# Sums of a GpSimd-added pair, issued later in TensorE's queue of a four-layer selective-scan kernel

## Chip, cores and metric

The kernel runs on one core of a Trainium2 chip. The metric is the device time of one execution in microseconds. The kernel before takes 22,061.91 us, the median of three runs (22,050.39 to 22,083.94).

## What is computed

Four layers are applied to a tensor of 4 images of 64x64 positions and 128 channels. Layers 0, 1 and 3 are selective-scan blocks, layer 2 is a gated block without a scan. The scan blocks take nearly all the time. Inside one, 256 channels are scanned along 4,096 positions in K = 4 directions, with N = 16 states for every channel:

```python
def step(h, t):
    dt_t, u_t, B_t, C_t = t
    h = h * jnp.exp(dt_t[..., None] * A) + (dt_t * u_t)[..., None] * B_t[:, :, None, :]
    y = jnp.einsum('bkdn,bkn->bkd', h, C_t)
    return (h, y)
```

So each state needs a decay (exp of delta times A), a driving term (delta times u times B, called the B product below), the recurrence itself, a multiplication by C, and the sum over the 16 states. Around the scans stand layer norms, projections, a 3x3 depthwise convolution, a gate and an MLP.

## The kernel before, in words

Twelve turns (4 images by 3 scan layers) are run, each with 4 directions of 8 chunks of 512 positions: 384 chunks. A chunk is cut into 8 periods, `i` = 0 to 7. A period has one group of four states (`q = i // 2`) and one half of the 256 channels on the 128 partitions. Two periods of the same `q`, an even one and the odd one after it, are called a pair here. There are 3,072 periods, 1,536 pairs.

The order of all instructions is written out by hand, in the loop over the periods (from L983). Each engine takes its instructions in that order. One period does this:

- ScalarE makes the decays of the next period (`decay`, L908), two states at a time ("sides" 0 and 1), and copies the driving term into PSUM (`lift`, L916).
- TensorE makes the B products of the first two states of the next period (`pair_db`, eight matmul instructions of L899 into the tile `dbp`, which has one buffer). VectorE makes those of the last two (L1048, L1049).
- VectorE runs four scans (L924), 128 x 512 each.
- GpSimd multiplies by C, two states in one instruction (`times_c`, L936, into a tile `hc` of four buffers). In even periods it then adds the two products of the sides (L938).
- TensorE sums over the states, by multiplying with an identity and accumulating in a PSUM bank for each half (`add_up`, L951; one sum is one call of it and two matmul instructions). An odd period has four sums (calls 0 to 3). An even one has two (calls 2 and 3), of the products that GpSimd has added. The last sum of a half appends it to the list `full`, and VectorE later takes the bank over (`leave`, L962 or L964).

In between stand the steps of other work, at four places in a period. `other(0)` stands after the first scan, `other(1)` after the B products of the next period, `other(2)` after the third scan and `other(3)` at the end. They hand out the norms, projections, MLP and convolution of the neighbouring turns, one kind of step at a time. A matmul step and the ScalarE, VectorE or GpSimd step that takes its result mostly stand at different places. All these matmuls write one PSUM tile, `gap`, with one buffer. `piece(2 * i)` after the B products and `piece(2 * i + 1)` at the end of a period give out the preparation of the next chunk (`prologue`, L814). Ten of the sixteen numbers have a piece; of those at the end of an odd period, number 3 (`i` = 1) has the projection `ps_x` (L835, in chunks of the forward directions), whose copy by ScalarE (L837) stands at the next place, and number 11 (`i` = 5) has four transposes of the tile `du` into `ps_duT` (L865), copied by ScalarE at L867.

On TensorE, from the B products issued in an odd period to those issued in the next even period, the order is: the pieces and steps of `other(1)` and `other(2)`; the two sums of the even period's pair (L951 x4 in the profile); the piece at the period's end and the steps of `other(3)`; in the next period the steps of `other(0)`; one sum of the odd period (L951 x2); the next B products (L899 x8). In the other half, at the end of an even period, three sums of the odd period before it stand together (L951 x6).

Of the kernel before, what the change touches and what calls it, by code (L numbers as in the profile page):

```python
# [77 lines left out]
def cost(step):  # L78

    return getattr(step, "matmuls", 0) or (0.05 if step is empty else 0.25)  # L80
# [6 lines left out]
def alike(a, b):  # L87
    return empty in (a, b) or hasattr(a, "matmuls") == hasattr(b, "matmuls")


def when(place):

    chunk, place = divmod(place - 1, 4 * len(ROOM))
    i, number = divmod(place, 4)
    return chunk + (sum(ROOM[:i]) + ROOM[i] * number / 4) / sum(ROOM)
# [3 lines left out]
def vss_stack_kernel(ctx: ExitStack, tc: tile.TileContext, x: bass.AP, weights, out: bass.AP, n_batch=B, layers=(0, 1, 2, 3)):  # L99
# [667 lines left out]
    for turn, (e, i) in enumerate(turns):  # L767

        for nth, k in enumerate((1, 3, 0, 2) if turn else (0, 1, 3, 2)):
            for ci in range(NCH):  # L770
                s = SimpleNamespace(turn=turn, e=e, v=wt[i], layer=i, nth=nth, k=k, ci=ci)
# [17 lines left out]
    def meanwhile(turn):  # L789

        chunk, end = 4 * 8, 4 * 8 * (per_turn - 2) - 4
        if not turn:

            first = [(row, n * chunk, (n + 1) * chunk - 2) for n, row in enumerate(opening[4:])]
            rest = combine(1, psums), combine(3, psums), *between(turns[1][0], None, 0, psums)
            return first + spaced(rest, first[-1][2], end)
        rows = after(*turns[turn - 1])
        if turn + 1 == len(turns):

            last = [(row, n * chunk + 8, (n + 1) * chunk + 8) for n, row in enumerate(after(*turns[turn]), 3 * NCH + 1)]  # L800
            return spaced(rows, 8, last[0][1]) + last
        if turns[turn + 1][1] == 0:
            rows += between(turns[turn + 1][0], None, 0, psums)
        return spaced(rows, 8, end)
# [4 lines left out]
    def scans(pool, ring, deep, psum):  # L809
# [60 lines left out]
        def spread(s, q, b):  # L870

            rows_of, at, count = ((s.bb, CQ * q + 2, CQ - 2), (s.cb, CQ * q, CQ))[b]
            rows_of[q] = pool.tile([P, count, CH], F32, tag="bc"[b] + "b", name="bc"[b] + "b")
            row = R + b * N + at
            nc.sync.dma_start(
                out=rows_of[q], in_=s.xd_d[s.k // 2 : s.k // 2 + 1, row : row + count].to_broadcast([P, count, CH])
            )

        def place(s, i):


            q = i // 2
            return q, (i + q + s.flip) % 2
# [19 lines left out]
        def decay(s, i, side):  # L903
            q, m = place(s, i)
            da = ring.tile([P, 2, CH], F32, tag="da", name="da")
            for j in range(2):
                n = CQ * q + 2 * side + j
                nc.scalar.activation(da[:, j], s.delta[:, m], AF.Exp, scale=s.v["a"][:, s.k, m, n : n + 1])  # L908
            return da
# [5 lines left out]
        def lift(s, i):  # L915
            nc.scalar.copy(dv[i % 2], s.du[:, place(s, i)[1]])  # L916

        def scan(s, i, side, j, da, db):
            q, m = place(s, i)
            if j == 0:  # L920
                s.h[i, side] = deep.tile([P, 2, CH], F32, tag="h", name="h")
            n = CQ * q + 2 * side + j
            init = 0.0 if s.first else s.state[:, m, n : n + 1]
            nc.vector.tensor_tensor_scan(  # L924
                s.h[i, side][:, j, s.step], da[:, j, s.step], db[:, s.step], init, ALU.mult, ALU.add
            )

        def save(s, i, side):
            if not s.last:
                q, m = place(s, i)  # L930
                n = CQ * q + 2 * side
                nc.scalar.copy(s.state[:, m, n : n + 2].unsqueeze(2), s.h[i, side][:, :, s.end : s.end + 1])  # L932
# [7 lines left out]
        def add_up(s, i, *calls):  # L940


            q, m = place(s, i)
            start, end = (0, 7) if m == s.flip else (1, 6)
            for call in calls:
                opens = i == start and call == (2 if i in PAIRED else 0)
                if opens:
                    setattr(s, f"yp{m}", psum.tile([P, CH], F32, tag=f"yp{m}", name="yp"))
                side, j = divmod(call, 2)
                closes = i == end and call == 3  # L950
                nc.tensor.matmul(getattr(s, f"yp{m}"), ident, s.hc[i, side][:, j], start=opens, stop=closes)  # L951
                if closes:
                    full.append((s, m))
# [17 lines left out]
        s = chunks[0]  # L971
# [9 lines left out]
        da = [decay(s, 0, side) for side in range(2)]  # L981
        pro = None
        periods = [(s, i) for s in chunks for i in range(8)]  # L983
        before, full = None, []
        for at, (s, i) in enumerate(periods):
            then = periods[at + 1] if at + 1 < len(periods) else None
            if i == 0:
                nxt = chunks[at // 8 + 1] if at // 8 + 1 < len(chunks) else None
                if nxt:
                    pro, nxt.dt = prologue(nxt), s.dt  # L990
                s.state = pool.tile([P, 2, N], F32, tag="state", name="state") if s.first else before[0].state
                if at % (8 * per_turn) == 0:
                    segments = [
                        SimpleNamespace(todo=steps, done=0, dense=True, total=len(steps), frm=frm, to=to)

                        if to - frm <= 4 * 8
                        else SimpleNamespace(
                            todo=steps, done=0, dense=False, total=sum(map(cost, steps)), frm=when(frm), to=when(to)
                        )
                        for steps, frm, to in meanwhile(s.turn)  # L1000
                    ]

            def piece(number):

                if nxt and number in PIECES:
                    next(pro)

            def other(number):

                place = at % (8 * per_turn) * 4 + number  # L1010
                for g in segments:
                    gone = place if g.dense else when(place)
                    while g.todo and g.done < g.total * (gone - g.frm) / (g.to - g.frm):
                        step = g.todo.pop(0)
                        g.done += 1 if g.dense else cost(step)
                        step()

                        if gone < g.to and not g.dense and (step is empty or g.todo and not alike(step, g.todo[0])):
                            break

            da_next = [None, None]
            spreads = (s, i // 2 + 1) if i < 7 else (nxt, 0)
            if i % 2 == 0 or not spreads[0]:
                spreads = None
            if then:
                da_next[0] = decay(*then, 0)
            if before:
                save(*before, 1)
            if spreads:
                spread(*spreads, 0)  # L1030
            scan(s, i, 0, 0, da[0], s.db[:, :, 0])
            other(0)
            scan(s, i, 0, 1, da[0], s.db[:, :, 1])
            times_c(s, i, 0)

            if before and i % 2 == 0:
                add_up(*before, 0)
            if then:
                pair_db(*then)
            piece(2 * i)  # L1040
            other(1)
            if spreads:
                spread(*spreads, 1)
            if then:
                da_next[1] = decay(*then, 1)
            save(s, i, 0)
            du, db = dv[i % 2], dv[1 - i % 2]
            nc.vector.tensor_mul(db, du, s.bb[i // 2][:, 0])  # L1048
            nc.vector.tensor_mul(du, du, s.bb[i // 2][:, 1])  # L1049
            scan(s, i, 1, 0, da[1], db)  # L1050
            other(2)
            scan(s, i, 1, 1, da[1], du)
            times_c(s, i, 1)
            if then:
                lift(*then)

            q, half = (i + 2 + i % 2) // 2, 1 - i % 2
            if q < 4:
                diagonals(s, q, half)
            elif nxt:  # L1060
                diagonals(nxt, q - 4, half)
            if i < 2 and full:
                leave(*full.pop(0))
            if before:
                add_up(*before, *((2, 3) if i % 2 else (1, 2, 3)))
            piece(2 * i + 1)
            other(3)
            da = da_next
            before = (s, i)
            if then and then[0].turn != s.turn:  # L1070
                assert not any(g.todo for g in segments)
        save(*before, 1)
        add_up(*before, 0, 1, 2, 3)
        while full:
            leave(*full.pop(0))
# [96 lines left out]
```

## Time and profile before

| what | value |
|---|---|
| median of three runs | 22,061.91 us |
| the profiled execution | 22,072.22 us |
| its span, first to last instruction | 22,070.4 us |
| granted TensorE clock, mean | 0.963 |
| VectorE busy | 19,479.8 us, 88% |
| GpSimd busy | 19,266.5 us, 87% |
| ScalarE busy | 18,587.9 us, 84% |
| TensorE (matmul) busy | 19,694.9 us, 89% |
| one pair of periods, span / 1,536 | 14.37 us |

How to read it: busy time is that of instructions on the engine itself; waiting at a semaphore is not in it. A line of the profile names a group of instructions by its line in the kernel, its engine and the tiles as output<-inputs. The view of the waits says which instruction sat idle before it started, what ended that idle time, how much in total, how often, and the longest one. PEld is the weight load that goes with a matmul.

### The profile page before, as it was taken

What the parts mean: (1) busy time and instruction counts of PE and PEld (TensorE: products, weight loads), DVE (VectorE), ACT (ScalarE), POOL (GpSimd) and SP (SyncE); (2) the same over time, 40 slices, a digit from 0 to 9 for tenths busy, and PEclk for the clock granted to TensorE, in tenths of its full rate; (3) what the DMA queues carried; (4) which work ended last, traced back from release to release, by engine and by line L of the source; (5) the groups of instructions that cost most, each with busy time, mean ns of one, the idle gap of its engine ahead of it and who ended that gap; (6) DMA issues with size and microseconds to landing.
All of it is one profiled execution on the core that took longest, in us unless ns stands there. A gap on an engine that the chain in (4) does not pass through costs nothing. (4 is left out here: it accounts for less than half of the span.)

```text
span 22070.4 us, 216982 instructions
## 1 busy us (share of the span) xinstructions
PE 19694.9 (89%) x58234; PEld 10511.8 (48%) x58234; DVE 19479.8 (88%) x20186; ACT 18587.9 (84%) x40022; POOL 19266.5 (87%) x8862
## 2 busy tenths in 40 slices
PE   7898998898889889889989988989988988898897
PEld 3444444444444444444444444444444444444443
DVE  5999999999888888899889899989988888889996
ACT  6888888888888888888888888888888888888887
POOL 5999899899888888888889888988988888889996
PEclk9999999999999999999999999999999999999999
DMA  4444444444335434434534544444443453354342
GB/s 109 147 149 146 135 144 149 136 139 151 130 131 139 142 128 140 146 133 145 144 138 144 145 141 140 141 147 134 142 149 127 137 143 137 131 140 145 140 144 101
DMA packets 2437559, 3060.10 MB, mean 139 GB/s; under 512 B 1753840, under 2 KB 1790064, under 8 KB 2238192
## 3 DMA queue, kind: packets, MB, share of 16 engines
q1 hardware_dynamic: 2436336, 3046.22, 44.4%
q8 instruction: 472, 7.73, 0.1%
q14 instruction: 751, 6.15, 0.1%
HBM read 2784.41 MB, written 261.49 MB: 138 GB/s over the span
## 5 line engine op out<-in xcount | busy, mean ns | idle before, releaser
L936 POOL TENSOR_TENSOR hc<-h,cb 128x1024 f32<-128x1024 f32 x6144 | 14399.4, 2363 | 2276.5 <-DVE h L924 1113.1
L951 PE MATMUL yp<-hc,ident 128*128 128x512 f32 x18432 | 9062.1, 618 | 688.3 <-POOL hc L938 546.8
L908 ACT ACTIVATE da<-delta,w 128x512 f32<-128x512 f32 x12288 | 8148.0, 713 | 543.5 <-DVE h L924 530.5
L924 DVE TENSOR_TENSOR_SCAN h<-da,state,dbp 128x512 f32<-128x512 f32 x5376 | 6573.3, 1262 | 818.9 <-PE dbp L899 576.0
L899 PE MATMUL dbp<-diag,duT 128*128 128x256 f32 x24576 | 6012.6, 388 | 652.4 <-DVE h L924 560.1
L924 DVE TENSOR_TENSOR_SCAN h<-da,state,dv 128x512 f32<-128x512 f32 x5376 | 6589.4, 1264 | 0.0
L899 PEld LDWEIGHTS dbp<-diag,duT 128*128 128x128 f32 x24576 | 4675.2, 193 | 2921.3 <-issue 1673.1
L951 PEld LDWEIGHTS yp<-hc,ident 128*128 128x128 f32 x18432 | 3483.6, 196 | 4999.1 <-issue 3656.8
L891 ACT ACTIVATE diag<-ident,bt 128x128 f32<-128x128 f32 x12288 | 3952.1, 402 | 0.0
L938 POOL TENSOR_TENSOR hc<-hc 128x1024 f32<-128x1024 f32 x1536 | 3624.1, 2359 | 120.4
L1048 DVE TENSOR_TENSOR dv<-dv,bb 128x512 f32<-128x512 f32 x3072 | 2088.3, 680 | 945.9 <-ACT dv L916 730.3
L916 ACT COPY dv<-du 128x512 f32<-128x512 f32 x3072 | 1799.1, 586 | 984.6 <-DVE h L924 977.1
L1049 DVE TENSOR_TENSOR dv<-dv,bb 128x512 f32<-128x512 f32 x3072 | 2118.4, 690 | 0.0
L444 PE MATMUL gap<-halo,cw 128*128 128x512 f32 x3456 | 1750.8, 604 | 5.9 <-DVE cen L281 2.2
L924 DVE TENSOR_TENSOR_SCAN h<-da,dbp 128x512 f32<-128x512 f32 x768 | 891.1, 1202 | 250.7 <-PE dbp L899 166.9
L859 POOL TENSOR_TENSOR du<-delta,xs 128x512 f32<-128x512 f32 x768 | 979.9, 1276 | 31.8 <-ACT delta L847 31.8
L842 PE MATMUL ps_dt<-xd,dt_w 8*128 8x512 f32 x1536 | 881.2, 654 | 130.2 <-ACT delta L845 78.2
L932 ACT COPY state<-h 128x2 f32<-128x2 f32 x5376 | 964.3, 179 | 0.0
L444 PEld LDWEIGHTS gap<-halo,cw 128*128 128x128 f32 x3456 | 628.1, 191 | 654.8 <-issue 617.8
L924 DVE TENSOR_TENSOR_SCAN h<-da,dv 128x512 f32<-128x512 f32 x768 | 893.8, 1204 | 0.0
L845 ACT ACTIVATE delta<-ps_dt,w 128x512 f32<-128x512 f32 x768 | 524.9, 683 | 103.0 <-PE ps_dt L842 98.2
L865 PEld LDWEIGHTS ps_duT<-ident,du 128*128 128x128 f32 x3072 | 383.7, 142 | 321.9 <-issue 255.8
(122 smaller groups left out, 11686.6 us busy)
## 6 DMA issues: line engine op xcount, KB each, us to landing
cb<-xd_d SPq DMA_DIRECT2D x1536, 1024.0 KB
bb<-xd_d SPq DMA_DIRECT2D x1536, 512.0 KB
xs<-x_row_d SPq DMA_DIRECT2D x192, 512.0 KB
xs<-x_col_d SPq DMA_DIRECT2D x192, 512.0 KB
x_col_d<-down SPq DMA_DIRECT2D x192, 256.0 KB
x_row_d<-wide SPq DMA_DIRECT2D x96, 512.0 KB
y_d<-y_sb SPq DMA_DIRECT2D x96, 512.0 KB
y<-y_d SPq DMA_DIRECT2D x96, 512.0 KB
```

Source lines behind the costliest of these rows:

```text
L444: nc.tensor.matmul(z.ps, z.cw[:, m, t, :], z.halo[c][:, dy : dy + RPC, dx : dx + W], start=(t == 0), stop=(t == 8),)
L859: nc.gpsimd.tensor_mul(s.du[:, m], s.delta[:, m], s.xs[:, m])
L891: nc.scalar.activation(s.diag[q][:, t, :, j], ident, AF.Copy, scale=s.bt[:, t, CQ * q + j : CQ * q + j + 1])
L899: nc.tensor.matmul(s.db[:, t * P : (t + 1) * P, :], s.duT[:, t, m, :], s.diag[q][:, t], start=True, stop=True)
L908: nc.scalar.activation(da[:, j], s.delta[:, m], AF.Exp, scale=s.v["a"][:, s.k, m, n : n + 1])
L916: nc.scalar.copy(dv[i % 2], s.du[:, place(s, i)[1]])
L924: nc.vector.tensor_tensor_scan(s.h[i, side][:, j, s.step], da[:, j, s.step], db[:, s.step], init, ALU.mult, ALU.add)
L936: nc.gpsimd.tensor_mul(hc, s.h[i, side], s.cb[i // 2][:, 2 * side : 2 * side + 2, :])
L938: nc.gpsimd.tensor_add(hc, hc, s.hc[i, 0])
L951: nc.tensor.matmul(getattr(s, f"yp{m}"), ident, s.hc[i, side][:, j], start=opens, stop=closes)
L1048: nc.vector.tensor_mul(db, du, s.bb[i // 2][:, 0])
L1049: nc.vector.tensor_mul(du, du, s.bb[i // 2][:, 1])
```

## The change

The two sums of an even period (calls 2 and 3) are no longer issued at the end of the odd period after it. They are issued in the following even period, after the steps of `other(0)`, directly before the one sum of the odd period that stood there already, and so directly before the next B products. Three sums now stand together there. To reach the pair two periods back, the loop keeps it in `earlier`. The first pair of the program is treated in the same manner as the others, and the last pair's sums follow the loop.

```diff
@@ -981,7 +981,7 @@
-        before, full = None, []
+        earlier, before, full = None, None, []
@@ -1033,7 +1033,8 @@
-            if before and i % 2 == 0:
+            if earlier and i % 2 == 0:
+                add_up(*earlier, 2, 3)
                 add_up(*before, 0)
             if then:
                 pair_db(*then)
@@ -1061,15 +1062,16 @@
             if i < 2 and full:
                 leave(*full.pop(0))
-            if before:
-                add_up(*before, *((2, 3) if i % 2 else (1, 2, 3)))
+            if before and i % 2 == 0:
+                add_up(*before, 1, 2, 3)
             piece(2 * i + 1)
             other(3)
             da = da_next
-            before = (s, i)
+            earlier, before = before, (s, i)
             if then and then[0].turn != s.turn:
                 assert not any(g.todo for g in segments)
         save(*before, 1)
+        add_up(*earlier, 2, 3)
         add_up(*before, 0, 1, 2, 3)
```

The number and kind of the instructions stay the same. The order changes on TensorE alone; VectorE, ScalarE, GpSimd and the queue of the transfers keep theirs.

## The prediction

> **What bounds the kernel now.** I read the page first.
>
> ```profile
> span 22070.4 us, 216982 instructions
> ...
> PE 19694.9 (89%) x58234; PEld 10511.8 (48%) x58234; DVE 19479.8 (88%) x20186; ACT 18587.9 (84%) x40022; POOL 19266.5 (87%) x8862
> ...
> L938 POOL TENSOR_TENSOR hc<-hc 128x1024 f32<-128x1024 f32 x1536 | 3624.1, 2359 | 120.4
> ```
>
> No engine is the bound alone: four stand between 84% and 89%. The time is set by how they wait for each other, so the view of the waits comes next (who waits <- for whom: us in total, times, longest).
>
> ```profile
> DVE h L924 <- PE dbp L899: 742.8, 557, 8.6
> DVE dv L1048 <- ACT dv L916: 730.3, 328, 7.5
> ...
> PE yp L951 <- POOL hc L938: 546.8, 361, 7.3
> ...
> ACT xd L837 <- PE ps_x L835: 248.3, 107, 8.4
> ...
> POOL hc L936 <- PE yp L951: 174.4, 97, 6.5
> ...
> PE yp L951 <- POOL hc L936: 121.9, 194, 1.2
> ...
> ACT duT L867 <- PE ps_duT L865: 104.9, 103, 5.2
> ```
>
> TensorE waits 546.8 us at the first of the sums that move, for GpSimd's addition. VectorE, which does the scans, waits mainly for TensorE's B products (742.8) and for ScalarE's copy (730.3). ScalarE is late in part because it waits for TensorE's preparation of the next chunk (248.3 and 104.9), whose matmuls stand right behind the sums that move. Two stretches of the timeline show both sides (start, us, engine, line; in brackets the idle time and what ended it). The first:
>
> ```profile
> 7114.69 3.78 PE L951 MATMUL yp<-hc,ident 128*128 128x512 f32 x4 [5.16 <-POOL hc L938]
> ...
> 7118.27 1.91 PE L696 MATMUL gap<-t,wg 128*128 128x512 f32 x2
> ...
> 7120.28 0.69 ACT L700 ACTIVATE c<-gap,wg 128x512 f32<-128x512 f32 x1 [5.02 <-PE gap L696]
> ...
> 7123.05 1.28 DVE L924 TENSOR_TENSOR_SCAN h<-da,state,dbp 128x512 f32<-128x512 f32 x1 [4.43 <-PE dbp L899]
> ```
>
> The sums wait 5.16 us for GpSimd; the step L696, which needs nothing of them, waits behind them; ScalarE waits for that step, and VectorE for the B products. The second:
>
> ```profile
> 7131.27 1.88 PE L951 MATMUL yp<-hc,ident 128*128 128x512 f32 x4
> ...
> 7133.71 1.13 PE L261 MATMUL gap<-res,mean 128*128 128x512 f32 x2 [0.56 <-POOL res L683]
> ...
> 7135.53 1.89 PE L899 MATMUL dbp<-diag,duT 128*128 128x256 f32 x8
> ...
> 7137.52 1.28 DVE L924 TENSOR_TENSOR_SCAN h<-da,state,dbp 128x512 f32<-128x512 f32 x1 [0.45 <-PE dbp L899]
> ```
>
> Here the sums are ready and fill 1.88 us in which the step L261 could not have run, since its input arrives at 7133.7. With the sums behind it, TensorE idles there, and the B products come 2.05 us later.
>
> **What the Trainium skill says.** "PSUM — Partial Sum Buffer", section Engine vs sequencer instructions: matmuls start and complete in program order, so a waiting matmul holds all matmuls behind it. The first stretch agrees: L696 follows the sums. "TensorE: Matmul & The Clock Gate", section What's actually happening: after an idle window of about 3.4 us TensorE's clock is halved until it has again been busy for such a time. The trace agrees: after the idle 5.16 us the four instructions take 3.78 us, against 1.88 us in the second stretch.
>
> **The change part by part.** No instruction is added or removed; 1,534 of the 1,536 pairs have a stretch that the change reorders. Per stretch it moves four matmul instructions (1.88 us) past the steps and a piece. I went through the trace's stretches, held all other engines where they are, and let each step start when the sums started waiting or its own input was written, whichever is later.
>
> What is there to move past: 402 stretches have no step or piece at all, so nothing changes in them; they hold 259 us of the 546 us of waiting. The other 1,132 have 2 to 12 matmul instructions.
>
> TensorE's own waits in these stretches, in us, by the odd period at whose end they lie (sum over its 383 or 384 chunks; "before" is at the moved sums + at the steps + at the third sum; "after" is at the steps + at the moved sums + at the third sum):
>
> i = 1: before 173+34+17 = 224; after 155+101+8 = 264.
> i = 3: before 66+36+0 = 102; after 151+45+1 = 197.
> i = 5: before 49+32+90 = 171; after 295+0+0 = 295.
> i = 7: before 259+73+32 = 364; after 213+172+46 = 431.
> Sum: before 861, after 1,187.
>
> So TensorE's waits are not taken away: that for GpSimd falls from 547 to 318, but the steps, 1.88 us earlier, wait 815 in place of 175 for ScalarE, VectorE and GpSimd. Net 326 us more. At i = 5 the transposes L865 wait for GpSimd's `du` or ScalarE's `bt`, 179 us.
>
> What reaches VectorE: the B products come over 0.15 us later in 293 stretches and earlier in 118. With the time that they now lie ready before VectorE takes them subtracted, VectorE starts later by 25+68+78+27 = 198 us (i = 1, 3, 5, 7), and its wait for them shrinks by 21+7+0+16 = 44 us. In the two periods after such a delay VectorE waits anyway for ScalarE, GpSimd or a transfer (mostly L1048 for L916); that absorbs half, and 11+17+54+16 = 98 us stay. I take 98, since the trace has those waits; the other end is 198.
>
> What the steps give: their results come up to 1.88 us plus the removed wait earlier. ScalarE's waits for them shrink by 363 us, 189 of it the projection (L837) and 86 the transposes (L867); VectorE's by 10, GpSimd's by 39. Followed along ScalarE's order until its next own wait, VectorE's waits for ScalarE (L1048, L924) shrink by 40 through L837, 17 through L867, and 25 through the takings L455, L524 and L277: 82 us.
>
> The clock: in 29 of the stretches with over 1.5 us of waiting for GpSimd a step was ready early enough to cut the idle time, and there the matmuls took 59 us more than at full clock. I take 59; bounds: 0, or a loss, since 326 us of new idle time can also halve the clock.
>
> The `hc` buffer of a pair is given back later: GpSimd's second product of the next even period reuses it. The sums now stand before B products that VectorE needs at the next period's start, about when that product may begin. Cost 0; bound: the excess of VectorE's waits over 2.1 us at those B products, 157 us. The bank of a finished half closes just before the B products, four scans before VectorE takes it (`leave`): 0, its waits being 12 us today. No transfer and no instruction of another queue is moved.
>
> Sum against the profiled execution: 22,072 + 98 - 44 - 82 - 59 = 21,985 us. The median of the runs is 10 us under the profiled execution, so 21,975 us, 0.4% less.
>
> **The rivals.** *Slower: the steps' waits decide.* The sums are then a filling that TensorE loses. Place: the stretches at i = 3 and 5. If nothing is absorbed and ScalarE's earlier results are lost to its next wait, the time is 22,062 + 198 - 44 = 22,216 us; if TensorE's 326 us count in full, 22,388. It decides where more than 185 us (44 + 82 + 59) of delay reach the end. For it: 815 against 175 us at the steps, and TensorE has the highest share, 89%. Against it: in half of the stretches VectorE takes its B products more than 0.7 us after they are ready.
>
> *Slower: buffers.* GpSimd waits for the later sums, up to 157 us: 22,219. Against it: today's waits of that kind are 174 us in only 97 cases.
>
> *No change.* The 363 us of ScalarE are followed by its waits for VectorE (977 us at L916) and vanish; gains and losses cancel: 22,062.
>
> *Faster by all of the 547 us*: 21,515. Against it: the 402 empty stretches, and 318 us that remain.
>
> That the change doesn't do what it says is excluded, since TensorE's order is seen to differ as described.
>
> **How the numbers follow.** About 0.2% (44 us) is what a measurement of this kernel can tell from no change. Faster through earlier steps, 0.45, likeliest, 21,975, own range 21,850 to 22,018. No change, 0.18. Slower through the steps' waits, 0.30, and through the buffers, 0.07. So faster 0.45, same 0.18, slower 0.37. The range for 8 in 10 goes from 21,860 (all gains, and no loss left but a few us: 22,062 - 185, with 17 more from GpSimd's 39) to 22,225, over both slower values; what lies beyond is the full 326 us.
>
> **What would show it.** Right: waits of L951 for L938 near 320 us, those of L837 for L835 near 60, more waits at L865, L540, L493, L274 and L521, VectorE's waits at L924 for `dbp` up by some 50 and at L1048 down by some 80, fewer long idle times of TensorE and a granted clock above 0.963. Wrong: L924's waits for `dbp` up by 150 or more, or L1048's not smaller (slower); L936's waits for L951 well above 174 (buffers).

## The result, and the profile after

The changed kernel takes 22,174.68 us, the median of 5 runs (22,161.0 to 22,179.94); the kernel before takes 22,061.91 us. The ratio is 1.0048, with a 95% interval of 1.0033 to 1.0062: 113 us slower. The forecast was 21,975 us, faster. Its 8-in-10 range (21,860 to 22,225 us) holds the measured time because it took in the slower rivals; the sum itself had the wrong sign.

The page of the changed kernel (a share of the span after each busy time):

```profile
span 22159.2 us, 216986 instructions
...
PE 19733.5 (89%) x58234; PEld 10519.6 (47%) x58234; DVE 19483.0 (88%) x20186; ACT 18595.3 (84%) x40022; POOL 19269.0 (87%) x8862
```

The work is the same: VectorE, ScalarE and GpSimd are busy within 8 us of before. The span of the traced execution grew by 88.8 us (the medians lie 113 us apart), and it grew by waiting: VectorE's time outside its work is up from 2,590.6 us (22,070.4 less 19,479.8) to 2,676.2 us. The view of the waits says which (who <- for whom: us in total, times, longest):

```profile
DVE h L924 <- PE dbp L899: 1016.5, 676, 8.7
...
DVE dv L1049 <- ACT dv L916: 631.9, 301, 6.5
...
POOL hc L936 <- PE yp L951: 343.6, 174, 7.7
PE yp L951 <- POOL hc L938: 303.7, 164, 5.8
```

L1049 is L1048 of before. TensorE's wait for GpSimd at the moved sums is down by 243 us, as the change means it to be, and yet the wait of VectorE for TensorE's B products is up by 274 us. VectorE's wait for ScalarE's copy is down by 98 us, and its other waits by some 90 us together, so that 86 of the 274 us are left in VectorE's total. GpSimd's wait for the sums is up by 169 us.

The two stretches of the timeline that the prediction showed, in the changed kernel. The first gained as expected:

```profile
7115.63 1.12 PE L696 MATMUL gap<-t,wg 128*128 128x512 f32 x2 [1.67 <-ACT t L288]
...
7116.59 1.88 PE L951 MATMUL yp<-hc,ident 128*128 128x512 f32 x4
...
7118.48 0.68 ACT L700 ACTIVATE c<-gap,wg 128x512 f32<-128x512 f32 x1
...
7121.89 1.28 DVE L924 TENSOR_TENSOR_SCAN h<-da,state,dbp 128x512 f32<-128x512 f32 x1
```

The step L696 runs while GpSimd is still adding; 5.16 us of waiting are 1.67 us now, ScalarE and VectorE no longer wait, and the sums run at full clock (1.88 us, not 3.78). The second lost, and by more than expected:

```profile
7132.54 1.12 PE L261 MATMUL gap<-res,mean 128*128 128x512 f32 x2 [2.27 <-POOL res L683]
...
7133.50 4.43 PE L951 MATMUL yp<-hc,ident 128*128 128x512 f32 x6
...
7137.77 1.89 PE L899 MATMUL dbp<-diag,duT 128*128 128x256 f32 x8
...
7139.77 2.45 DVE L924 TENSOR_TENSOR_SCAN h<-da,state,dbp 128x512 f32<-128x512 f32 x2 [3.86 <-PE dbp L899]
```

TensorE waits 2.27 us for the input of L261, which the sums had covered before. The three sums then take 4.43 us. Before, they took 1.88 us, which the prediction shows, and 1.02 us in this line of the kernel before:

```profile
7134.67 1.02 PE L951 MATMUL yp<-hc,ident 128*128 128x512 f32 x2
```

VectorE waits 3.86 us for the B products, where it waited 0.45 us. From the start of L261 to the B products it was 1.82 us, and is 5.23 us.

### The profile page after: what moved, and what is told of

It reads as the page before. It is cut to its first block, busy times and chain, and to the rows that moved or that the text cites. A ratio compares the mean times of both kernels' runs of the same rounds, so it can differ in the third digit from the quotient of the medians.

```text
span 22159.2 us, 216986 instructions
## 1 busy us (share of the span) xinstructions
PE 19733.5 (89%) x58234; PEld 10519.6 (47%) x58234; DVE 19483.0 (88%) x20186; ACT 18595.3 (84%) x40022; POOL 19269.0 (87%) x8862
## 5 line engine op out<-in xcount | busy, mean ns | idle before, releaser
L936 POOL TENSOR_TENSOR hc<-h,cb 128x1024 f32<-128x1024 f32 x6144 | 14398.8, 2362 | 2388.9 <-DVE h L924 1046.9
L951 PE MATMUL yp<-hc,ident 128*128 128x512 f32 x18432 | 8877.5, 616 | 381.5 <-POOL hc L938 303.7
L908 ACT ACTIVATE da<-delta,w 128x512 f32<-128x512 f32 x12288 | 8147.6, 713 | 635.0 <-DVE h L924 621.2
L924 DVE TENSOR_TENSOR_SCAN h<-da,state,dbp 128x512 f32<-128x512 f32 x5376 | 6571.4, 1261 | 984.9 <-PE dbp L899 802.2
L924 DVE TENSOR_TENSOR_SCAN h<-da,state,dv 128x512 f32<-128x512 f32 x5376 | 6585.6, 1263 | 0.0
L899 PE MATMUL dbp<-diag,duT 128*128 128x256 f32 x24576 | 5989.8, 387 | 556.7 <-DVE h L924 484.1
L899 PEld LDWEIGHTS dbp<-diag,duT 128*128 128x128 f32 x24576 | 4668.5, 193 | 2790.0 <-issue 1495.0
L951 PEld LDWEIGHTS yp<-hc,ident 128*128 128x128 f32 x18432 | 3514.6, 197 | 4838.8 <-issue 3844.0
L938 POOL TENSOR_TENSOR hc<-hc 128x1024 f32<-128x1024 f32 x1536 | 3624.2, 2360 | 120.5
L1049 DVE TENSOR_TENSOR dv<-dv,bb 128x512 f32<-128x512 f32 x3072 | 2084.6, 679 | 856.3 <-ACT dv L916 631.9
L916 ACT COPY dv<-du 128x512 f32<-128x512 f32 x3072 | 1799.0, 586 | 1081.8 <-DVE h L924 1076.8
L444 PE MATMUL gap<-halo,cw 128*128 128x512 f32 x3456 | 1729.9, 607 | 27.2 <-ACT wide L426 11.5
L924 DVE TENSOR_TENSOR_SCAN h<-da,dbp 128x512 f32<-128x512 f32 x768 | 890.2, 1200 | 264.4 <-PE dbp L899 214.3
L444 PEld LDWEIGHTS gap<-halo,cw 128*128 128x128 f32 x3456 | 626.5, 191 | 678.6 <-issue 604.1
L924 DVE TENSOR_TENSOR_SCAN h<-da,dv 128x512 f32<-128x512 f32 x768 | 892.7, 1201 | 0.0
L865 PE MATMUL ps_duT<-ident,du 128*128 128x128 f32 x3072 | 475.8, 278 | 225.4 <-POOL du L859 162.5
```

Of the source, the lines that this page charges most:

```text
L444: nc.tensor.matmul(z.ps, z.cw[:, m, t, :], z.halo[c][:, dy : dy + RPC, dx : dx + W], start=(t == 0), stop=(t == 8),)
L899: nc.tensor.matmul(s.db[:, t * P : (t + 1) * P, :], s.duT[:, t, m, :], s.diag[q][:, t], start=True, stop=True)
L924: nc.vector.tensor_tensor_scan(s.h[i, side][:, j, s.step], da[:, j, s.step], db[:, s.step], init, ALU.mult, ALU.add)
L936: nc.gpsimd.tensor_mul(hc, s.h[i, side], s.cb[i // 2][:, 2 * side : 2 * side + 2, :])
L938: nc.gpsimd.tensor_add(hc, hc, s.hc[i, 0])
```

## The experiments

Two theories stood at the start. **A**: the steps, now first, wait for inputs that the sums used to cover, the sums follow late, and the B products behind them come late to VectorE. **B**: GpSimd's product buffers are given back later, which the growth from 174 to 344 us speaks for. Times before are the median of all runs of the kernel before on the same chip.

**One end at a time.** In a chunk the sums move at the ends of i = 1, 3, 5 and 7. Four kernels move them at one end only; the two lines at the top shift the later line numbers by two and more.

```diff
+MOVED = (1,)        # or (3,), (5,), (7,)
...
-                add_up(*earlier, 2, 3)
+                if before[1] in MOVED:
+                    add_up(*earlier, 2, 3)
                 add_up(*before, 0)
...
                 add_up(*before, 1, 2, 3)
+            elif before and i not in MOVED:
+                add_up(*before, 2, 3)
             piece(2 * i + 1)
...
```

> The two sums go behind the steps only at the end of i = 1 (384 of the 1,536 pairs); elsewhere they stay as before. Theory A (the steps, now first, wait for their inputs and the next B products come later at VectorE): the stretches at i = 1 gave VectorE 21 us less and 25 us more waiting for B products, and ScalarE 189 us less for the projection, of which 40 us reach VectorE; so about 40 us faster, 22,020 us, within 21,990 to 22,060. Theory B (the buffers of GpSimd's products come free later): GpSimd's waits for the sums grew by 43 us at i = 2, so about 30 us slower, 22,090 us.

> The sums go behind the steps only at the end of i = 3. Theory A: VectorE's wait for the B products of i = 5 grew by 148 us with the whole change, part of it absorbed by its wait for ScalarE's copy in the same period; 60 to 100 us slower, about 22,140 us. Theory B: GpSimd's waits for the sums grew by 89 us at i = 4; 60 to 90 us slower too, so this run alone does not tell the two apart by its time, but its trace does: which of the two waits is there.

> The sums go behind the steps only at the end of i = 5, where the transposes L865 now wait for GpSimd's du. Theory A: VectorE's wait for the B products of i = 7 grew by 87 us; 40 to 80 us slower, about 22,120 us. Theory B: GpSimd's waits for the sums at i = 6 grew by 9 us only; within 15 us of before, 22,060 us.

> The sums go behind the steps only at the end of i = 7. Theory A: VectorE's waits for the B products of i = 1 grew by 27 us; 0 to 25 us slower, about 22,075 us. Theory B: GpSimd's waits for the sums grew by 37 us at i = 0; about 30 us slower, 22,090 us.

| moved at the end of | time, us (before 22,068.55) | ratio, 95% interval |
|---|---|---|
| i = 1 | 22,056.53 | 0.9996 (0.9988 to 1.0005) |
| i = 3 | 22,077.18 | 1.0005 (0.9997 to 1.0013) |
| i = 5 | 22,141.15 | 1.0036 (1.0023 to 1.0048) |
| i = 7 | 22,127.00 | 1.0026 (1.0016 to 1.0036) |

The four differences add up to 128 us (-12 + 9 + 73 + 58), about the whole change's 113 us. The loss is made at i = 5 and i = 7. At i = 5 the time is what theory A expected, and not what B expected, which was nothing. At i = 1 both missed: A expected about 40 us less, B 30 us more, and the 12 us measured are not clear of nothing. At i = 3 both expected a loss and both missed. The waits of that run show why:

```profile
DVE h L926 <- PE dbp L901: 848.2, 580, 8.7
...
DVE dv L1052 <- ACT dv L918: 655.6, 302, 6.5
...
POOL hc L938 <- PE yp L953: 261.6, 127, 7.3
ACT xd L839 <- PE ps_x L837: 236.2, 104, 8.3
```

(These are L924 for L899, L1048 for L916, L936 for L951 and L837 for L835 of before.) VectorE waits 105 us more for B products, but 75 us less for ScalarE's copy. Both happen in the periods i = 5, which take the delayed B products: there the first wait rises from 155 to 295 us, and the second falls from 262 to 190 us. ScalarE's copy is late in these periods in any case, and so a good part of the delay is absorbed. GpSimd waits 87 us more for the sums, and that costs nothing that can be measured. At i = 7 the loss of 58 us is larger than A (at most 25 us) and B (about 30 us) expected.

**More buffers.** Five buffers for the products in place of four, in both kernels. The cut leaves out the edits that make room: five weight matrices of the gated layer are read from parts of other weight tiles, so that layer computes other values; the number of instructions of each engine stays.

```diff
-            hc = s.hc[i, side] = deep.tile([P, 2, CH], F32, tag="hc", name="hc")
+            hc = s.hc[i, side] = prods.tile([P, 2, CH], F32, tag="hc", name="hc")
...
+        tc.tile_pool(name="prods", bufs=5) as prods,
...
```

> The changed kernel with five buffers for GpSimd's products in place of four, so that the buffer of an added pair is needed again one product later. To make room, five weight matrices of the gated layer (w1, wse, w2, wf1, wf2) are read from parts of other layers' weight tiles in place of their own, so that layer's values differ; instructions, shapes and order stay. Theory B (buffers): GpSimd's waits for the sums (344 us in the changed kernel) nearly vanish and the time goes back towards 22,070 us, 70 us or more under the changed kernel. Theory A (later B products): GpSimd's waits vanish too, but VectorE's waits for B products stay near 1,000 us and the time stays over 22,140 us; the same distance to the kernel before with five buffers as without, about 0.4 to 0.5%.

> The kernel before with the same five buffers and the same replaced weights of the gated layer, to compare the run above with. Both theories: GpSimd's waits for the sums (174 us) vanish. Theory A: within 0.15% of before, since those waits lie beside others. Theory B: up to 0.5% faster.

Measured, against 22,067.48 us: the changed kernel 22,158.53 us, 1.0038 (1.0024 to 1.0053); the kernel before 22,074.80 us, 1.0003 (0.9994 to 1.0011). The two lie 84 us apart. The waits of the changed kernel with five buffers (lines are shifted by five):

```profile
DVE h L929 <- PE dbp L904: 956.4, 651, 9.6
...
POOL hc L941 <- PE yp L956: 146.6, 98, 11.7
```

And of the kernel before with five:

```profile
DVE h L929 <- PE dbp L904: 757.0, 553, 9.8
...
POOL hc L941 <- PE yp L956: 100.4, 73, 5.6
```

GpSimd's waits for the sums did not vanish as expected, but fell to 147 us, under the 174 us of the original kernel, and the time stayed. VectorE's waits for the B products stayed high, at 956 us. Theory B is refuted as the main cause; a share of up to the 29 us between 113 and 84 us can't be told from none.

**Which of the two places.** For i = 5 the first guess was the transposes L865, which in the changed kernel wait for GpSimd's `du`. Two kernels part them from the steps, and a third parts the two places at i = 7. The first puts the sums of i = 5 behind the piece alone:

```diff
-            if before:
+            if before and i != 5:
                 add_up(*before, *((2, 3) if i % 2 else (1, 2, 3)))
             piece(2 * i + 1)
+            if before and i == 5:
+                add_up(*before, 2, 3)
             other(3)
```

The second has `other(3)` ahead of the sums at i = 5, and the piece behind them. The third has the sums of i = 7 behind `other(3)`, at the end of their period.

> The kernel before, with the two sums at the end of i = 5 moved behind the piece alone (the transposes L865 of du), ahead of all steps. If the transposes' wait for GpSimd's du and ScalarE's bt, which the sums covered, is what cost 73 us when the sums went behind piece and steps there: 50 to 75 us slower, about 22,130 us. If the steps of the two places are the cause: within 20 us of before, 22,067 us.

> The kernel before, with the steps of the last place of i = 5 put in front of the two sums; the transposes stay behind the sums and keep their cover. If the transposes' wait is the cause: within 25 us of before, 22,067 us. If the steps are: 30 us or more slower, 22,100 us.

> The kernel before, with the two sums at the end of i = 7 moved behind the steps of that place only, ahead of the steps of the next chunk's first place, which has the most steps (its share of the time is 2.8, the others' 1 to 1.8). If the loss at i = 7 (58 us) comes from the steps of the next chunk's first place: within 20 us of before, 22,067 us. If it comes from those at the end of i = 7: 40 us or more slower, 22,110 us.

Measured, against 22,070.17 us: 22,065.67 us, 0.9999 (0.9990 to 1.0008); 22,082.68 us, 1.0005 (0.9996 to 1.0013); 22,067.94 us, 0.9998 (0.9990 to 1.0007). So the transposes alone are not it, though their wait is there in full in the first of these kernels (L865 for `du`; before 0.0 us):

```profile
PE ps_duT L865 <- POOL du L859: 164.8, 120, 6.5
```

Nor is it the steps of the period's last place alone: 13 us, not clear of nothing, where 30 us or more were expected. At i = 7 the 58 us are gone when the sums stay ahead of the next period's first place, `other(0)`. Then the same at all four ends:

```diff
-            if before:
-                add_up(*before, *((2, 3) if i % 2 else (1, 2, 3)))
+            if before and i % 2 == 0:
+                add_up(*before, 1, 2, 3)
             piece(2 * i + 1)
             other(3)
+            if before and i % 2:
+                add_up(*before, 2, 3)
```

> The two sums of all odd ends moved behind the piece and the steps of the last place, but ahead of the steps of the next period's first place: one of the two places of the change. If it is the first place of the next period whose steps lose their cover right ahead of the B products: within 30 us of before, 22,067 us, VectorE's wait for B products at most 60 us over 743, and TensorE's waits at the steps of that first place as in the kernel before (62 us at i = 7). If each of the two places takes its share: 50 us or more slower, 22,120 us. If bringing sums close to the B products is what costs, whatever stands between: 80 us or more slower, 22,150 us.

Measured 22,077.98 us against 22,061.22, 1.0006 (0.9997 to 1.0015): 17 us, not clear of nothing, where the full change has 113. The two kernels have the same order wherever the next period's first place has no step, which is so in 1,089 of the 1,535 stretches (the prediction counted 1,534); what parts them lies in the other 446. The waits:

```profile
DVE h L924 <- PE dbp L899: 794.3, 572, 10.0
DVE dv L1048 <- ACT dv L916: 692.5, 316, 6.5
...
PE yp L951 <- POOL hc L938: 350.3, 212, 7.3
...
POOL hc L936 <- PE yp L951: 254.4, 119, 10.0
```

TensorE's wait for GpSimd has lost four fifths of what it loses in the full change (196 of 243 us), and VectorE's wait for the B products has grown by 52 us, not 274. This kernel also shows in its order which steps belong to the next period's first place, so that TensorE's waits between two groups of B products can be counted apart in every trace (us over all stretches; idle time ahead of each matmul):

| kernel | at the pieces and earlier steps | at the sums | at the steps of the next period's first place | together |
|---|---|---|---|---|
| before | 231 | 685 | 145 | 1,061 |
| changed | 485 | 382 | 423 | 1,290 |
| first place only | 522 | 415 | 133 | 1,070 |
| only i = 7 moved | 261 | 608 | 248 | 1,117 |
| only past ready work (below) | 248 | 610 | 146 | 1,004 |

Moved past the first of the two places, TensorE trades a wait at the sums for one at the steps, and the sum stays (1,061 and 1,070 us): the sums still run while ScalarE, VectorE and GpSimd make the inputs of the steps that follow. Moved past the second place too, nothing is left between those steps and the ones before them. Their waits rise from 133 to 423 us, those at the sums fall by 33 us only, and right behind stand the B products. This is theory A, at one place.

What the runs show is this place. The way from there to the end of the kernel is shown in part. With i = 5 alone VectorE waits 144 us more for B products (887.2 us), and its wait for ScalarE's copy absorbs nothing (724.7 against 730.3 us). But the total of that wait doesn't measure the loss: it is up by 58 us behind the transposes alone and by 105 us at i = 3, at no loss that is clear of nothing. At i = 7, where 58 us are lost, it is up by 17 us only:

```profile
DVE h L926 <- PE dbp L901: 759.9, 572, 8.7
```

The steps of the first place wait longer at i = 1 and i = 3 too (by 59 and 78 us, each end moved alone). At i = 3 the absorption above explains why that costs little; for i = 1 it stays open.

**What an earlier result for ScalarE is worth.** The sums at i = 1 go behind the projection `ps_x` alone.

```diff
-            if before:
+            if before and i != 1:
                 add_up(*before, *((2, 3) if i % 2 else (1, 2, 3)))
             piece(2 * i + 1)
+            if before and i == 1:
+                add_up(*before, 2, 3)
```

> The kernel before, with the two sums moved behind the piece alone at the end of i = 1 (the projection ps_x, whose input is always there), but ahead of all steps. No filling is lost. Theory A: ScalarE's wait at L837 falls from 248 to about 60 us, nothing else waits longer; 20 to 50 us faster, about 22,035 us. Rival: ScalarE's earlier copy vanishes in its next wait for VectorE, as with the sums behind all steps at i = 1 (12 us, within its uncertainty): no change, 22,065 us.

Measured 22,053.48 us against 22,067.48, 0.9994 (0.9985 to 1.0002): 14 us less at the median, not clear of nothing, where theory A expected 20 to 50 us. The waits, behind one line of the kernel before:

```profile
ACT dv L916 <- DVE h L924: 977.1, 1124, 4.0
```

```profile
ACT dv L916 <- DVE h L924: 1023.3, 1175, 4.2
DVE h L924 <- PE dbp L899: 749.5, 548, 8.7
...
DVE dv L1048 <- ACT dv L916: 730.4, 328, 7.5
...
ACT xd L837 <- PE ps_x L835: 79.5, 33, 5.4
```

ScalarE waits 169 us less at L837. It waits 46 us more for VectorE at L916 and 42 us more at L908 (572.7 against 530.5 us), and VectorE's wait for ScalarE at L1048 is 730.4 us, where it was 730.3. ScalarE's gain did not reach VectorE there.

**A version that moves only past ready work.** The sums go behind the taps of the convolution (L444) and the projection, whose inputs are there, and ahead of any other matmul step.

```diff
+            def release():
+                while held:
+                    add_up(*held.pop(0), 2, 3)
...
+                if number == 11:             # in piece(): the transposes
+                    release()
...
                         step = g.todo.pop(0)
+                        if hasattr(step, "matmuls") and not hasattr(step, "ready"):
+                            release()
...
             if before and i % 2 == 0:
+                release()
                 add_up(*before, 0)
...
-            if before:
-                add_up(*before, *((2, 3) if i % 2 else (1, 2, 3)))
+            if before and i % 2 == 0:
+                add_up(*before, 1, 2, 3)
+            elif before:
+                held.append(before)
...
+                    taps.ready = True
                     S.append(taps)
...
```

> At all odd ends the sums move, but only past work whose inputs are there already: the taps of the convolution (L444) and the projection ps_x; they are issued ahead of any other matmul step, ahead of the transposes at i = 5, and at the latest where the change has them. Theory A: TensorE keeps its filling, so VectorE's waits for B products stay within 50 us of 743; a part of the wait for GpSimd and most of ScalarE's wait at L837 go; 30 to 80 us faster, about 22,010 us. Theory B: GpSimd's waits for the sums grow in the stretches with a convolution; no gain, 22,065 us or slower.

Measured 22,046.94 us against 22,067.48, 0.9990 (0.9983 to 0.9997): 21 us faster, the only version that beats the kernel before by more than its uncertainty, by less than expected. Its waits (lines shifted by one, from L1048 on by ten):

```profile
DVE h L925 <- PE dbp L900: 772.5, 558, 8.8
DVE dv L1058 <- ACT dv L917: 723.3, 325, 7.5
...
PE yp L952 <- POOL hc L939: 451.7, 290, 7.2
...
ACT xd L838 <- PE ps_x L836: 77.8, 32, 5.5
```

95 us of TensorE's wait for GpSimd are gone, and VectorE's wait for B products is 30 us over the 743 us of before. Which of the smaller waits makes the 21 us isn't shown.

## Why the prediction was wrong

**TensorE's waits: right.** The wait for L938 was forecast near 320 us and is 304; L837's near 60 us and is 77. In the stretches the waits at the steps were to grow by 640 us and grew by 532 (376 to 908, the steps ahead of the sums counted in); those at the sums were to shrink by 313 us and shrank by 303. Net 326 us were forecast, 229 are there. That 402 stretches have nothing to move past, and that part of the wait for GpSimd stays, held.

**What reaches VectorE: undersized.** Waits for B products were to grow by 198 - 44 = 154 us before absorption, and grew by 274. Absorption was real: 98 of the 274 us, where half was forecast, stand at L1049, 75 of them in the periods i = 5. The forecast for the single ends, after absorption and the smaller wait, was -10, 10, 54 and 0 us for i = 1, 3, 5 and 7; measured were -12, 9, 73 and 58. For i = 1 and 3 this is agreement within intervals of some 18 us on either side, and that the figures lie within 2 us of each other is luck. At i = 7 the term failed by its full size: next to nothing was forecast, and 58 us were lost. With the sums of i = 7 moved the trace shows only 17 us more of waiting at L924 for B products. That execution was also the fastest of its eight, 22,103 us; what makes the rest of the 58 us stays open.

**The gains: the step that failed.** The sum took off 82 us for ScalarE's earlier results, which were to shorten VectorE's waits for ScalarE, and 59 us for the clock. Neither is in the result; these 141 us are the larger part of the 200 us between forecast and measurement.

ScalarE's results do come earlier, but the step from there to VectorE fails. The run that moves the sums behind the projection alone shows it: ScalarE's wait for the projection falls by 169 us, VectorE's wait at L1048 not at all, and ScalarE waits 88 us more for VectorE. The prediction forecast a fall by some 80 us at L1048 as a sign of being right, and 98 us are there, but for another reason: 86 of them lie in the periods i = 5 and 7, whose B products come late, and the run with i = 3 alone has 75 us of them with L837 nearly unchanged (236 against 248 us). The wait fell since it absorbed a delay, not since a gain arrived.

As for the clock, matmul instructions that took over 1.3 times the median of their group lost 782 us before and 834 us after, and the granted clock is 0.960 in place of 0.963, where it was to rise. The long waits that went are paid for by the new ones, as the stretch with 4.43 us for three sums shows. The rise is there with i = 5 alone (831 us), and not with i = 7 alone (781 us) or with the first place only (782 us). So at i = 5 the lost filling and the slower clock come together, and no run parts them.

Without these two terms the sum gives 22,062 + 98 - 44 = 22,116 us with the absorption and 22,216 us without; the measured 22,175 lies between.

**The rivals.** The slower one, through the steps' waits, was the right mechanism, and its sign came: L924's waits for the B products rose by more than 150 us. Its place was named as i = 3 and 5; it is i = 5 and 7, and within the stretch it is the steps of the next period's first place. Its point of decision, 185 us of delay, was too high, since two of the three gains it had to outweigh were not there. The rival of no change was right on ScalarE's gains, which vanish in its waits for VectorE. Through the buffers 169 us of waiting came, a little over the bound of 157 us, at little or no cost. The banks that VectorE takes over late, put at nothing, made it wait 31 us in place of 12.

## What to carry to other kernels

Work that can wait is worth something in an in-order queue as filling: it covers the time in which others make the input of what follows it. Before moving it, count for each instruction that it is moved past whether its input is there already, and what stands right behind; here it paid only past work that was ready, and cost most where the steps stood directly ahead of what the busiest engines waited for. And an earlier result is a gain only if it arrives: follow it to the engine that counts, since here ScalarE's shorter wait for TensorE came back in good part as a longer wait for VectorE. A wait that gets shorter isn't proof of a gain either, as it may have absorbed a delay.

## What was not expected of the hardware

The clock's part in short waits. In the second stretch of the changed kernel the granted clock fell to half. The view of windows gives each engine's busy time, and behind it the granted clock, the DMA share and GB/s:

```profile
7130.40:7133.80 3.40, 1.26 (x3) 0.68 (x4) 3.40 (x5) 3.40 (x8) 2.86 (x3) 1.00 0.14 51
7133.80:7137.20 3.40, 3.40 (x5) 1.35 (x4) 2.11 (x3) 3.37 (x6) 3.40 (x3) 0.50 0.84 228
```

TensorE had idled 2.27 us ahead of L261, less than the about 3.4 us that the prediction names; here the measurement decides. The six instructions of the sums took 4.43 us in place of 2.90. This is no rare case. The clock of the kernel before was halved 331 times, and in 231 of them no single idle time that reached into the last 3.4 us was as long as 3.4 us. In the changed kernel it was halved 357 times. It ran at half for 1,650 us before and for 1,791 us after, in a kernel whose TensorE is busy 89% of the span. The 782 us of slow instructions before are 3.5% of the span; the ends of matmul instructions are modelled, so this is an estimate.
